# A perceiver layer on one core: context groups turned by TensorE, score sums taken inside the products, sums moved between VectorE, GpSimd and ScalarE

## The chip, the core and the metric

The kernel runs on one core of a Trainium2 chip. The metric is the device time of one execution in microseconds (us), as the median of several runs. The core's engines have a queue each and run side by side: TensorE (PE in the profile, its weight loads PEld), VectorE (DVE), ScalarE (ACT), GpSimd (POOL) and SyncE (SP), which here only issues DMAs. Everything is float32.

## The reference, cut to what matters

A layer of three parts works on 256 query tokens `x` of width 512: a cross attention with 25,088 context tokens, a causal self attention with 16 heads, and a mixture of experts. The change lies in the first part:

```python
x = x + _L0_xattn_ref(_layernorm(x), ctx_1024, ctx_1024, Wq, bq, Wk, bk, Wv, bv)

def _L0_xattn_ref(q, k, v, Wq, bq, Wk, bk, Wv, bv):
    qp = q @ Wq.T + bq            # 256 x 128
    kp = k @ Wk.T + bk            # 25088 x 128
    vp = v @ Wv.T + bv            # 25088 x 512
    z = sigmoid(qp @ kp.T / sqrt(128))   # 256 x 25088, no softmax
    return z @ vp
```

Since no softmax is taken, `z @ (ctx @ Wv.T + bv)` is `(z @ ctx) @ Wv.T + rsum * bv`, where `rsum` is the sum of each query's row of `z`. The kernel computes `z @ ctx` over all tokens, projects once at the end, and needs `rsum` for the bias.

## The kernel before

**The loop over groups.** The context is cut into 66 groups. Group 0 has 128 tokens (one block), each of groups 1 to 65 has 384 (three blocks of 128). For each group `g` the kernel does this:

- `load_quarters(g)` (line 119, four DMAs) loads the tokens cut into quarters of 512 bytes over the partitions, and `load_context(g)` (line 128) loads them again as they are, tokens on partitions. Both are issued by SP, three groups ahead in the loop; there are 3 buffers of quarters and 5 of context.
- `turn(g)` (line 315) turns the quarters on VectorE, by blocks of 32 x 32, into `cT`, with model width on partitions. Group 0 alone goes another way: `turn_by_pe(0)` (lines 317 to 329) turns its block from the context tile with four TensorE transposes and one ScalarE copy. The quarters have another order of rows than a plain transpose, so `keys` takes the weights `wkT_sb` for them, and `wk_plain_sb` for group 0.
- `keys(g)` (line 339) multiplies `cT` by the key weights, and ScalarE adds the bias (line 348). This gives `kT`.
- `scores` (line 360) multiplies `kT` by the queries `qT`, and ScalarE writes the sigmoid as `zT` (line 369), tokens on partitions.
- `context_sums` and `query_sums` (line 501) form sums of parts, and `values` (line 527) multiplies them. Here `z @ ctx` is a product of 2 x 3 blocks (`a00` to `a12`: two halves of the queries by three token blocks) and 3 x 3 blocks (`b00` to `b22`: three token blocks by three thirds of the width, 172 or 170 columns). A scheme with 15 products in place of 18 is used: each product `p0` to `p14` multiplies a block or sum of blocks of `zT` (`s0` to `s9`) by a block or sum of blocks of the context (`t0` to `t12`). The 15 products are summed over all groups in six PSUM banks. The `s` sums are all on VectorE; of the 13 `t` sums VectorE makes 6 and GpSimd 7.
- `summed` (line 379) adds the whole `zT` to `zsum` on GpSimd, for `rsum`.

**The order of the work.** Each engine's instructions run in program order. In iteration `g` the program issues, per engine:

- PE: scores of `g` for two blocks, the first four products of group `g-1`, scores for the third block, keys of `g+1`, the other eleven products of `g-1`
- DVE: `t` sums of `g`, `s` sums of `g`, turn of `g+2`
- POOL: seven `t` sums of `g`, then `zsum`, and in five groups some one-element copies (line 159) that hold back the DMAs of later weights
- ACT: the two sigmoids of `g`, the bias of `kT` for `g+1`

`t` sums have two buffers, so those of group `g` can be written only when the products of `g-2` have been read.

**Start and end.** Before the loop PE warms up (line 244), turns group 0 (line 324) and the normalised `x` (line 555), computes the keys of group 0 and the queries (line 565); on VectorE `turn(1)` stands ahead of `qT` (line 575). After the loop the last products run, ScalarE copies five of the six banks to SBUF (line 624), and the 15 products are combined into the six blocks `c00` to `c12` of the result by 21 additions (line 645), six of them on GpSimd. The first half is turned by PE (line 652), copied by ACT (line 657) and projected (line 690), then the second half. `rsum` comes from `zsum`: two GpSimd additions (lines 609 and 610), PE products with a column of ones (line 666), and a copy (line 675), used at line 679.

Of the kernel before, what the change touches and what calls it, by code (L numbers as in the profile page):

```python
# [14 lines left out]
P = 128  # L15
# [6 lines left out]
def tile_perceiver_layer(  # L22
# [84 lines left out]
    def blocks_of(g):  # L107

        return range(J) if g > 0 else (1,)
# [23 lines left out]


    x_sb = act.tile([P, NT, D], F32, tag="x", name="x_sb")
    for t, queue in enumerate((nc.sync, nc.scalar)):
# [5 lines left out]
    bq_sb = load("bq", [QK, 1], bq, queue=nc.gpsimd)  # L142
    load_quarters(1)
    wkT_sb = const.tile([P, ND, QK], F32, tag="wkT", name="wkT_sb")
    for a in range(NA):
# [3 lines left out]
        )  # L149
    load_context(1)  # L150

# [165 lines left out]
    def turn_by_pe(g):  # L317

        cT = new_turned(g)
        pt = sum_bank(f"ptc_{g}")  # L320
        ct = ctx_tiles[g][:, 1, :]
        for c in range(ND):
            chunk = slice(c * P, (c + 1) * P)
            in_turn(nc.tensor.transpose(pt[:, chunk], ct[:, chunk], ident))
        in_turn(
            nc.scalar.copy(
                cT[:, :, 0 : P // R, :], pt.rearrange("p (c b r) -> p c b r", c=ND, r=R)
            )
        )

    def keys(g):

        cT = turned_tiles.pop(g)
        n = len(blocks_of(g)) * P
        w = wkT_sb if g > 0 else wk_plain_sb
        pk = keys_bank(f"pk_{g}")[:, 0:n]
        for c in range(ND):
            in_turn(
                nc.tensor.matmul(  # L339
                    pk,  # L340
                    lhsT=w[:, c, :],
                    rhs=cT[:, c, 0 : n // R, :].rearrange("p b r -> p (b r)"),
                    start=(c == 0),
                    stop=(c == ND - 1),
                )
            )
        kT = cpool.tile([QK, J * P], F32, tag="kT", name=f"kT_{g}")
        in_turn(nc.scalar.activation(kT[:, 0:n], pk, AF.Identity, bias=bk_sb))  # L348
        return kT

    zsum = cpool.tile([P, J, T], F32, tag="zsum", name="zsum", bufs=1)
    nc.gpsimd.memset(zsum, 0.0)

# [22 lines left out]

    def summed(g, zT):
        part = slice(blocks_of(g)[0], blocks_of(g)[-1] + 1)
        in_turn(nc.gpsimd.tensor_add(zsum[:, part, :], zsum[:, part, :], zT[:, part, :]))  # L379

# [24 lines left out]
        t11 b02 - t0  # L405
        t12 b11 + t7
        t8 t2 + t4
    """
    T_SUMS_BY_POOL = """
        t1 b10 + b12  # L410
        t3 t1 - b22
        t4 b20 - t3
        t9 b02 + t1
        t5 b12 - b22
        t10 t5 - b11
        t6 b11 - b02
    """

    PRODUCTS = (
        ("p6 s2 t3", "p14 s0 t8", "p8 s5 b11"),  # L420
        ("p13 s6 b02", "p11 s8 t6"),
        ("p5 a12 b20", "p1 a01 t10", "p7 s1 t2"),
        ("p0 s9 b22", "p9 a00 t11"),
        ("p10 a10 b00", "p4 s7 b21"),
        ("p12 s4 t9", "p3 a11 b10", "p2 s3 t12"),
    )
    FIRST_S_SUMS = "s4 a11 + a01"
    FIRST_T_SUMS = """
        t1 b10 + b12
        t10 b12 - b11  # L430
    """
    FIRST_PRODUCTS = (
        ("p6 a01 t1", "p8 a11 b11"),
        ("p11 s4 b11",),
        ("p1 a01 t10",),
        (),
        (),
        ("p12 s4 t1", "p3 a11 b10"),
    )

    RESULTS = """
# [3 lines left out]
        u9 u6 - p7  # L445
        u13 p1 + u1
        u2 u1 - p9
        | u15 u9 - p5
        u4 p1 + u2
        | c02 p0 + u13  # L450
        u8 p7 - p10
        c01 u2 - p4
        | c00 u15 - u4
        u3 p2 + p4
        u11 p12 - p0
        | u7 p8 + u3
        u5 p3 + p13
        u10 p3 + p5
        | u14 u11 - p6
        c10 p10 + u10  # L460
        c11 u7 + u8
        | c12 u14 - u5
    """

    WIDE = ("p2", "p4", "p7", "p8", "p9", "p10", "p11", "p13")
    NS_SUMS, NT_SUMS, NU_SUMS = 10, 13, 16
    product, banks_of_products = {}, []

    def open_products():
        for i, names in enumerate(PRODUCTS):  # L470
            held = sum_bank(f"xacc_{i}")
            banks_of_products.append(held)
            at = 0
            for text in names:
                nm = text.split()[0]
                width = WIDTH if nm in WIDE else WIDTH - 2
                product[nm] = (i, slice(at, at + width))
                at += width

    class Named:  # L480


        def __init__(self, g):
            self.g = g
            self.s = self.t = self.z = None

        def __getitem__(self, nm):
            kind, at = nm[0], nm[1:]
            if kind == "a":
                i, k = int(at[0]), int(at[1])  # L490
                return self.z[:, k, i * P : (i + 1) * P]
            if kind == "b":
                lo = third_at[int(at[1])]
                return ctx_tiles[self.g][:, int(at[0]), lo : lo + WIDTH]
            return (self.s if kind == "s" else self.t)[:, int(at), :]

    def do_sums(engine, text, named):
        for line in text.strip().splitlines():
            to, x_, op, y_ = line.split()
            f = engine.tensor_add if op == "+" else engine.tensor_sub  # L500
            in_turn(f(named[to], named[x_], named[y_]))  # L501

    def context_sums(g, named):
        named.t = cpool.tile([P, NT_SUMS, WIDTH], F32, tag="T", name=f"T_{g}")
        if g == 0:
            do_sums(nc.vector, FIRST_T_SUMS, named)
        else:
            do_sums(nc.gpsimd, T_SUMS_BY_POOL, named)
            do_sums(nc.vector, T_SUMS, named)

# [6 lines left out]
    def values(named, lo=0, hi=15):  # L517
        g = named.g
        made = [
            (i, text.split(), text is names[-1])  # L520
            for i, names in enumerate(PRODUCTS if g > 0 else FIRST_PRODUCTS)
            for text in names
        ]
        for i, (nm, lhs, rhs), last in made[lo:hi]:
            cols = product[nm][1]
            in_turn(
                nc.tensor.matmul(  # L527
                    banks_of_products[i][:, cols],
                    lhsT=named[lhs],
                    rhs=named[rhs][:, 0 : cols.stop - cols.start],  # L530

# [27 lines left out]
    for i, copy in enumerate((nc.vector.tensor_copy, nc.scalar.copy)):  # L559
        in_turn(copy(xnT[:, 2 * i : 2 * i + 2, :].rearrange("p c t -> p (c t)"), pxs[i]))  # L560
    kT = keys(0)
    pq = sum_bank("pq")
    for c in range(ND):
# [8 lines left out]
        )  # L572
    turn(1)
    qT = cpool.tile([QK, T], F32, tag="qT", name="qT", bufs=1)
    in_turn(nc.vector.tensor_scalar(qT, pq[:, :T], bq_sb, None, ALU.add))  # L575
    open_products()
    load_quarters(2)
    load_context(2)


    before = None
    for g in range(G):
        if g + 3 < G:
            load_quarters(g + 3)
            load_context(g + 3)
        named = Named(g)
        named.z = zT = cpool.tile([P, J, T], F32, tag="zT", name=f"zT_{g}", bufs=3)
# [11 lines left out]
        query_sums(g, named)  # L599
        if g + 2 < G:  # L600
            turn(g + 2)
        summed(g, zT)
        for fetch in in_group.get(g, ()):
            fetch(zT[0:1, 0, 0:1])
        before = named
    values(before)


    in_turn(nc.gpsimd.tensor_add(zsum[:, 0, :], zsum[:, 0, :], zsum[:, 1, :]))
    in_turn(nc.gpsimd.tensor_add(zsum[:, 0, :], zsum[:, 0, :], zsum[:, 2, :]))  # L610

# [14 lines left out]
    def result(nm):  # L626
        if nm[0] == "p":
            i, cols = product[nm]
            widths[nm] = cols.stop - cols.start
            return banks_of_products[i][:, cols] if i == len(PRODUCTS) - 1 else held[i][:, cols]  # L630
# [5 lines left out]
    for line in RESULTS.strip().splitlines():  # L636
        engine = nc.gpsimd if "|" in line else nc.vector
        to, x_, op, y_ = line.replace("|", "").split()
        a_, b_, o_ = result(x_), result(y_), result(to)
        n = widths[to] = min(widths[x_], widths[y_])  # L640
        assert to not in ("c01", "c11") or n == WIDTH
        if to[0] == "c" and to[2] != "1":
            n = WIDTH - 2
        f = engine.tensor_add if op == "+" else engine.tensor_sub
        in_turn(f(o_[:, 0:n], a_[:, 0:n], b_[:, 0:n]))
    zcT = work.tile([P, ND, T], F32, tag="tokT", name="zcT")

# [14 lines left out]
    turn_zc(0, sum_bank)  # L662
    pr = sum_bank("pr")
    for t in range(NT):
        in_turn(
            nc.tensor.matmul(
                pr[:, t : t + 1],
                lhsT=zsum[:, 0, t * P : (t + 1) * P],
                rhs=ones_sb,
                start=True,  # L670
                stop=True,
            )
        )
    rsum = act.tile([P, NT], F32, tag="rsum", name="rsum")
    in_turn(nc.vector.tensor_copy(rsum, pr[:, 0:NT]))
    x1 = act.tile([P, NT, D], F32, tag="x1", name="x1")
# [854 lines left out]
```

## Time and profile before

| What | us |
|---|---|
| median of 3 runs | 795.2 (793.04 to 795.24) |
| the profiled execution, its own time | 796.75 |
| its span, first to last instruction | 794.9 |
| PE busy | 775.6 (98%) |
| DVE busy | 636.8 (80%) |
| POOL busy | 400.1 (50%) |
| ACT busy | 157.8 (20%) |
| DMA | 141.62 MB, 178 GB/s over the span |

The profiled execution is 1.85 us longer than its span, and 1.55 us longer than the median of the runs. The span falls into these stages by the timeline: start to the keys of group 3 at 30.47 us; the even loop to the keys of group 65 at 541.48 us; its end, with the last products, to about 561.2 us; the projection, self attention and experts to 794.9 us. Busy times on PE are modelled at their ends, and a VectorE instruction whose record is stretched counts as busy for all of it.

### The profile page before, as it was taken

Reading aid. Unit: us, or ns where it says so; the run is one execution under the profiler, and the core shown is the slowest. Engines: PE = TensorE matmul, PEld = TensorE weight load, DVE = VectorE, ACT = ScalarE, POOL = GpSimd, SP = SyncE. Lnnn points to the kernel's source line nnn. Section 1 sums busy time; section 2 is a strip of 40 time slices with the busy share of each in tenths; the row PEclk is TensorE's granted clock in tenths of the full one; section 3 lists DMA queues with packets and bytes.
Section 4 is the critical chain, followed back from the end, with each engine's and each line's share of the span. In section 5 each row is a group of like instructions: output and inputs, shape, how many; then the busy total and the mean of one; then the engine's idle time right before and its main releaser. Section 6 shows DMA issues by size and latency. Waiting matters only on the chain.

```text
span 794.9 us, 11690 instructions
## 1 busy us (share of the span) xinstructions
PE 775.6 (98%) x3994; PEld 609.6 (77%) x3994; DVE 636.8 (80%) x1389; ACT 157.8 (20%) x350; POOL 400.1 (50%) x574
## 2 busy tenths in 40 slices
PE   7999999999999999999999999999999899999996
PEld 4788888888888888888888888888675586775562
DVE  4899999999999999999999999999556463512222
ACT  2211112111121121212111121111445220110110
POOL 4576767767676676767767677676323000000000
PEclk8999999999999999999999999999999999999999
DMA  9998997997778787777878778730510033399400
GB/s 241 269 238 215 304 228 231 247 232 209 183 195 202 172 212 175 206 191 184 206 169 210 185 196 198 170 113 1 190 50 1 0 133 111 127 353 393 154 2 30
DMA packets 155251, 141.62 MB, mean 178 GB/s; under 512 B 9137, under 2 KB 114609, under 8 KB 155185
## 3 DMA queue, kind: packets, MB, share of 16 engines
q1 hardware_dynamic: 154448, 140.28, 66.7%
q8 instruction: 34, 0.56, 0.3%
q10 hardware_dynamic: 672, 0.52, 0.2%
q14 instruction: 33, 0.26, 0.1%
q0 software_dynamic: 64, 0.00, 0.0%
HBM read 140.25 MB, written 0.52 MB: 177 GB/s over the span
## 4 chain that ended last, share of the span: by engine, by line
DVE 52%; PE 40%; DMA 3%; issue 2%; POOL 1%; ACT 1%; SPq 0%; DVEq 0%; POOLq 0%; ACTq 0%
DVE T L501 27%; DVE S L501 13%; DVE cT L315 11%; PE xacc L527 7%; PE ph_e L1089 7%; PE pk L339 5%; PE pd_e L1136 3%; DMA quarters<-in_context 3%; PE ph_s L1089 3%; PE pz L360 2%; PE pd_s L1136 2%; PE pa L804 2%; PE ph_few L1358 1%; PE pw L868 1%; PE py L690 1%
## 5 line engine op out<-in xcount | busy, mean ns | idle before, releaser
L501 POOL TENSOR_TENSOR T<-ctx 128x172 f32<-128x172 f32 x195 | 124.0, 636 | 143.7 <-PE xacc L527 143.7
L501 DVE TENSOR_TENSOR T<-ctx,T 128x172 f32<-128x172 f32 x195 | 190.6, 1003 | 2.2
L339 PE MATMUL pk<-cT,wkT_sb 128*128 128x384 f32 x520 | 181.3, 492 | 0.9 <-DVE cT L315 0.8
L527 PE MATMUL xacc<-T,S 128*128 128x170 f32 (+1 forms) x782 | 167.4, 309 | 0.9 <-DVE S L501 0.9
L527 PEld LDWEIGHTS xacc<-T,S 128*128 128x128 f32 x782 | 134.1, 191 | 21.6 <-POOL zsum L379 1.2
L339 PEld LDWEIGHTS pk<-cT,wkT_sb 128*128 128x128 f32 x520 | 96.6, 192 | 61.3 <-DVE cT L315 2.5
L379 POOL TENSOR_TENSOR zsum<-zsum,zT 128x768 f32<-128x768 f32 (+1 forms) x66 | 123.9, 1877 | 14.4 <-ACT zT L369 14.4
L369 ACT ACTIVATE zT<-pz 128x256 f32<-128x256 f32 (+1 forms) x131 | 64.1, 489 | 286.1 <-PE pz L360 282.7
L315 DVE STREAM_TRANSPOSE cT<-quarters 128x1536 f32<-128x1536 f32 x65 | 115.1, 1771 | 5.8 <-DMA quarters<-in_context 5.8
L360 PE MATMUL pz<-qT,kT 128*128 128x256 f32 x392 | 106.7, 381 | 3.7 <-DVE qT L575 2.8
L527 PE MATMUL xacc<-ctx,S 128*128 128x172 f32 (+1 forms) x522 | 108.9, 310 | 0.4 <-DVE S L501 0.4
L527 PE MATMUL xacc<-ctx,zT 128*128 128x170 f32 (+1 forms) x394 | 89.5, 309 | 0.0
L527 PEld LDWEIGHTS xacc<-ctx,S 128*128 128x128 f32 x522 | 85.0, 191 | 0.9 <-DVE S L501 0.9
L501 DVE TENSOR_TENSOR T<-ctx 128x172 f32<-128x172 f32 x132 | 81.5, 618 | 0.0
L501 DVE TENSOR_TENSOR S<-zT,S 128x128 f32<-128x128 f32 x325 | 78.8, 292 | 0.0
L360 PEld LDWEIGHTS pz<-qT,kT 128*128 128x128 f32 x392 | 68.8, 190 | 8.9 <-issue 3.2
L501 POOL TENSOR_TENSOR T<-T,ctx 128x172 f32<-128x172 f32 x130 | 67.5, 519 | 10.2
L501 POOL TENSOR_TENSOR T<-ctx,T 128x172 f32<-128x172 f32 x130 | 65.9, 528 | 5.1
L348 ACT ACTIVATE kT<-pk,bk 128x384 f32<-128x384 f32 (+1 forms) x66 | 38.1, 577 | 151.9 <-PE pk L339 151.9
L527 PEld LDWEIGHTS xacc<-ctx,zT 128*128 128x128 f32 x394 | 66.3, 191 | 0.0
L501 DVE TENSOR_TENSOR S<-zT 128x128 f32<-128x128 f32 x196 | 57.9, 296 | 3.3 <-ACT zT L369 3.3
L527 PE MATMUL xacc<-T,zT 128*128 128x170 f32 (+1 forms) x264 | 60.2, 310 | 0.0
(238 smaller groups left out, 722.0 us busy)
## 6 DMA issues: line engine op xcount, KB each, us to landing
quarters<-in_context SPq DMA_DIRECT2D x260, 192.0 KB, 5.0
ctx<-in_context SPq DMA_DIRECT2D x65, 768.0 KB, 5.3
gu<-in_e_gate_up SPq DMA_DIRECT2D x12, 1024.0 KB, 7.3
dn<-in_e_down SPq DMA_DIRECT2D x11, 512.0 KB, 4.9
gu_s<-in_s_gate_up SPq DMA_DIRECT2D x8, 512.0 KB, 6.3
a_wqT<-in_a_wqT SPq DMA_DIRECT2D x1, 2048.0 KB, 8.1
a_wout<-in_a_woutT SPq DMA_DIRECT2D x1, 2048.0 KB, 9.2
dn_s<-in_s_down SPq DMA_DIRECT2D x4, 512.0 KB, 8.3
```

What stands on the lines that cost most here:

```text
L315: in_turn(nc.vector.transpose(new_turned(g), q.rearrange("p b (c r) -> p c b r", r=R)))
L339: nc.tensor.matmul(pk, lhsT=w[:, c, :], rhs=cT[:, c, 0 : n // R, :].rearrange("p b r -> p (b r)"), start=(c == 0), stop=(c == ND - 1),)
L348: in_turn(nc.scalar.activation(kT[:, 0:n], pk, AF.Identity, bias=bk_sb))
L360: nc.tensor.matmul(pz[:, i * T : (i + 1) * T], lhsT=kT[:, at : at + P], rhs=qT, start=True, stop=True,)
L369: nc.scalar.activation(zT[:, blocks[0] : blocks[-1] + 1, :].rearrange("p j t -> p (j t)"), pz[:, 0 : len(blocks) * T], AF.Sigmoid, scale=1 ...
L379: in_turn(nc.gpsimd.tensor_add(zsum[:, part, :], zsum[:, part, :], zT[:, part, :]))
L501: in_turn(f(named[to], named[x_], named[y_]))
L527: nc.tensor.matmul(banks_of_products[i][:, cols], lhsT=named[lhs], rhs=named[rhs][:, 0 : cols.stop - cols.start],  start=i not in opened, ...
L690: nc.tensor.matmul(pys[t], lhsT=zcT[:, c, t * P : (t + 1) * P], rhs=wvT_sb[:, c, :], start=(c == 0), stop=(c == ND - 1),)
L804: nc.tensor.matmul(pa[:, 0 : hi - lo], lhsT=a_wqT_sb[:, c, e * P : (e + 1) * P], rhs=anT[:, c, lo:hi], start=(c == 0), stop=(c == ND - 1),)
L1089: nc.tensor.matmul(ph[:, f * T + lo : f * T + hi], lhsT=gu[:, c, col : col + P], rhs=fT[:, c, lo:hi], start=(c == 0), stop=(c == ND - 1),)
L1136: nc.tensor.matmul(pd, lhsT=hT[:, f, t * P : (t + 1) * P], rhs=dn[:, f, :], start=(f == 0), stop=(f == NI - 1),)
```

## The change

**Start.** Groups 0 and 1 (`BY_PE = 2`) are turned by TensorE. `turn_by_pe` now takes groups of three blocks: 12 transposes into four PSUM banks, each bank copied out by ACT or DVE in turn. The quarters of group 1 are not loaded; its context is loaded where its quarters were, and the quarters of group 2 come next. `qT` comes ahead of the turn of group 1 on its engines. `keys(1)` takes `wk_plain_sb`. One sigmoid of a single column is put behind the copies of `xnT` on ScalarE.

**Score sums.** The `t` tiles are two fixed ones, 174 columns wide, whose last columns are set to 1.0 once. The products `p0`, `p9`, `p10` and `p12` get one more column, which reads a one: it sums the product's `s` or `a` operand over the tokens. `p0` and `p10` used a block of the context itself, which has no ones beside it, so ScalarE copies these two blocks to `t13` and `t14`. `summed`, `zsum` and all that made `rsum` of it are taken out; `rsum` is three one-column operations on VectorE.

**The sums.** `t5`, `t10` and `t6` go from GpSimd to VectorE: 9 there, 4 on GpSimd. GpSimd's four and ScalarE's two copies for group `g+1` are issued at the end of iteration `g` (`context_sums_aside`). `t1` shares the place of `t10`. The products are laid out in the banks anew, and issued in another order of banks except in the last group.

**End.** The 21 additions of the result are all on VectorE, in another order.

The diff, cut to its core:

```diff
+    BY_PE = 2
...
-    load_quarters(1)
+    load_context(1)
+    load_quarters(2)
     wkT_sb = const.tile([P, ND, QK], F32, tag="wkT", name="wkT_sb")
...
-    load_context(1)
+    load_context(2)
...
     def turn_by_pe(g):
         cT = new_turned(g)
...
+        blocks = blocks_of(g)
+        n = len(blocks)
+        many = 512 // (n * P)
+        for lo in range(0, ND, many):
+            pt = sum_bank(f"ptc_{g}_{lo}")[:, 0 : many * n * P]
+            for c in range(lo, lo + many):
+                for i, k in enumerate(blocks):
+                    at = ((c - lo) * n + i) * P
+                    in_turn(
+                        nc.tensor.transpose(
+                            pt[:, at : at + P],
+                            ctx_tiles[g][:, k, c * P : (c + 1) * P],
+                            ident,
+                        )
+                    )
+            to = cT[:, lo : lo + many, 0 : n * P // R, :]
+            src = pt.rearrange("p (c b r) -> p c b r", c=many, r=R)
+            if lo % 2:
+                in_turn(nc.vector.tensor_copy(to, src))
+            else:
+                in_turn(nc.scalar.copy(to, src))
...
-        w = wkT_sb if g > 0 else wk_plain_sb
+        w = wkT_sb if g >= BY_PE else wk_plain_sb
...
-    def summed(g, zT):
-        part = slice(blocks_of(g)[0], blocks_of(g)[-1] + 1)
-        in_turn(nc.gpsimd.tensor_add(zsum[:, part, :], zsum[:, part, :], zT[:, part, :]))
...
     T_SUMS = """
...
+        t5 b12 - b22
+        t10 t5 - b11
+        t6 b11 - b02
         t8 t2 + t4
     """
     T_SUMS_BY_POOL = """
         t1 b10 + b12
         t3 t1 - b22
+        t9 b02 + t1
         t4 b20 - t3
-        t9 b02 + t1
-        t5 b12 - b22
-        t10 t5 - b11
-        t6 b11 - b02
     """
+    T_COPIES_BY_ACT = "t13 b22, t14 b00"
...
-        ("p0 s9 b22", "p9 a00 t11"),
-        ("p10 a10 b00", "p4 s7 b21"),
-        ("p12 s4 t9", "p3 a11 b10", "p2 s3 t12"),
+        ("p9 a00 t11", "p4 s7 b21"),
+        ("p12 s4 t9", "p3 a11 b10", "p0 s9 t13"),
+        ("p10 a10 t14", "p2 s3 t12"),
     )
...
-        ("p12 s4 t1", "p3 a11 b10"),
+        ("p12 s4 t9", "p3 a11 b10", "p0 a01 t13"),
...
+    BANK_ORDER, LAST_ORDER = (0, 1, 2, 4, 3, 5), range(6)
+    SCORE_SUMS = ("p0 + p9", "p12 - p0 + p10")
+    WITH_ONES = ("p0", "p9", "p10", "p12")
...
-                width = WIDTH if nm in WIDE else WIDTH - 2
+                width = (WIDTH if nm in WIDE else WIDTH - 2) + (nm in WITH_ONES)
...
+    t_tiles = []
+    for i in range(2):
+        t = cpool.tile([P, NT_SUMS, WIDTH + 2], F32, tag=f"T{i}", name=f"T_{i}", bufs=1)
+        nc.vector.memset(t[:, :, WIDTH - 2 :], 1.0)
+        t_tiles.append(t)
+    nc.vector.memset(t_tiles[0][:, 13, 0 : WIDTH - 2], 0.0)
...
+    def context_sums_aside(g, named):
+        if g == 0:
+            return
+        do_sums(nc.gpsimd, T_SUMS_BY_POOL, named)
+        for line in T_COPIES_BY_ACT.split(", "):
+            to, x_ = line.split()
+            n = WIDTH - 2 if to in NARROW_T else WIDTH
+            in_turn(nc.scalar.copy(named[to][:, 0:n], named[x_][:, 0:n]))
...
+    warm = small.tile([P, 1], F32, tag="warm", name="warm_0", bufs=1)
+    in_turn(nc.scalar.activation(warm, eps_sb, AF.Sigmoid))
     kT = keys(0)
...
-    turn(1)
     qT = cpool.tile([QK, T], F32, tag="qT", name="qT", bufs=1)
     in_turn(nc.vector.tensor_scalar(qT, pq[:, :T], bq_sb, None, ALU.add))
+    turn_by_pe(1)
     open_products()
-    load_quarters(2)
-    load_context(2)
...
         query_sums(g, named)
-        if g + 2 < G:
+        if BY_PE <= g + 2 < G:
             turn(g + 2)
-        summed(g, zT)
         for fetch in in_group.get(g, ()):
             fetch(zT[0:1, 0, 0:1])
-        before = named
+        before, named = named, Named(g + 1)
+        if g + 1 < G:
+            context_sums_aside(g + 1, named)
     values(before)
-    in_turn(nc.gpsimd.tensor_add(zsum[:, 0, :], zsum[:, 0, :], zsum[:, 1, :]))
-    in_turn(nc.gpsimd.tensor_add(zsum[:, 0, :], zsum[:, 0, :], zsum[:, 2, :]))
...
-        engine = nc.gpsimd if "|" in line else nc.vector
...
+    rsum = act.tile([P, NT], F32, tag="rsum", name="rsum")
+    for t, text in enumerate(SCORE_SUMS):
...
+            in_turn(f(rsum[:, t : t + 1], total, result(nm)[:, -1:]))
...
-    pr = sum_bank("pr")
-    for t in range(NT):
-        in_turn(
-            nc.tensor.matmul(
-                pr[:, t : t + 1],
-                lhsT=zsum[:, 0, t * P : (t + 1) * P],
-                rhs=ones_sb,
...
-    in_turn(nc.vector.tensor_copy(rsum, pr[:, 0:NT]))
```

## The prediction

> **What bounds the kernel now.** I read the chain of waits first, because busy shares alone (PE 98%, VectorE 80%) don't say which engine sets the pace. Then the windows by stage, then the timeline of one group and of both ends.
>
> The chain names VectorE for half of the span and PE for most of the rest. In an early stretch it stays on PE for a whole group (start, length, what):
>
> ```profile
> 38.97 2.58 PE pk L339 x8
> 41.55 3.19 PE xacc L527 x22
> 44.74 0.86 PE pz L360 x4
> 45.60 1.16 PE xacc L527 x8
> 46.76 0.43 PE pz L360 x2
> ```
>
> These five pieces follow each other without a gap and add up to 8.22 us. That is PE's own work for a group. The windows (length, then busy time of PE, PEld, DVE, ACT, POOL, then clock and DMA):
>
> ```profile
> 11.08:13.92 2.84, 0.01 (x2) 0.03 (x1) 2.29 (x3) 0.00 (x0) 0.00 (x0) 0.88 1.08 312
> 13.92:20.22 6.30, 6.29 (x10) 3.13 (x10) 2.16 (x4) 0.38 (x1) 4.19 (x8) 0.51 1.16 272
> ...
> 30.47:541.48 511.01, 510.92 (x2729) 431.62 (x2730) 506.74 (x1055) 96.35 (x185) 355.61 (x504) 1.00 0.81 202
> ...
> 553.06:561.21 8.15, 6.80 (x30) 5.97 (x30) 5.69 (x15) 2.51 (x5) 3.52 (x5) 0.79 0.00 0
> ```
>
> Over the even loop PE is busy 510.92 of 511.01 us and VectorE 506.74: both are full. The keys of group 3 start it and those of group 65 end it, so it holds 62 groups at 511.01/62 = 8.242 us, 0.02 over PE's own 8.22. So PE is the floor, and VectorE just keeps up. The other rows show PE idle or at half clock, at both ends. VectorE's fullness is partly waiting, as the timeline of one group shows:
>
> ```profile
> 181.00 2.48 DVE L501 TENSOR_TENSOR T<-ctx,T 128x172 f32<-128x172 f32 x2
> 181.38 1.90 POOL L379 TENSOR_TENSOR zsum<-zsum,zT 128x768 f32<-128x768 f32 x1
> ...
> 183.40 0.33 DVE L501 TENSOR_TENSOR T<-T 128x172 f32<-128x172 f32 x1
> 183.65 0.28 DVE L501 TENSOR_TENSOR S<-zT 128x128 f32<-128x128 f32 x1
> ```
>
> Two sums take 2.48 us beside `zsum`; with GpSimd quiet, one starts 0.25 us after another (183.40, 183.65), and an `S` sum 0.20 us (177.16, 177.36).
>
> **The change part by part.** I count against the profiled execution (796.75 us; span 794.9).
>
> *Start.* In the timeline the queries end on PE at 11.08, and then:
>
> ```profile
> 11.62 1.78 DVE L315 STREAM_TRANSPOSE cT<-quarters 128x1536 f32<-128x1536 f32 x1 [2.99 <-DMA quarters<-in_context]
> ...
> 13.33 0.44 DVE L575 TENSOR_SCALAR qT<-pq,bq 128x256 f32<-128x256 f32 x1
> ```
>
> `qT` stands behind the turn of group 1, which waits for quarters. PE idles 2.83 us, its clock falls to half, and keys of group 1 take 5.12 us instead of 2.58. After the change `qT` is ready at 11.55. The context of group 1 (0.77 MB) is the fifth load, after 1.3 MB; with the 207 GB/s of the first window, 2.1 MB are there at 10.2 us. Bounds: 9.5, at the rate of other context loads (about 2.2 us each beside 3.5 for a group's quarters), and 11.6, when the quarters landed in that place. I take 10.2. From 11.08 PE makes 12 transposes at 0.11 each (the four of group 0 and the four at 562.27 both), 1.4 us. Each bank's copy costs ACT or DVE about 0.5 (0.59 for 512 columns); two each, the first three under the transposes. PE then runs pz of group 0 (0.43), keys 1 (2.58, from 12.95), a gap for kT (0.65, as before), pz 0.86, four products 1.16, pz 0.43: keys 2 at 18.65. Those need turn 2: its quarters landed at 18.7 before, behind those of group 1, `wkT` and the context; now they follow the context by 3.3 us of DMA, at 13.5, so `cT` is ready at about 15.6, and `wkT` lands at about 15.5. Then keys 2.58, three products 0.87, pz 0.86, four products 1.16, pz 0.43: keys 3 at 24.55. Turn 3 needs quarters that landed at 24.4 before; 0.77 MB less ahead of them makes 21.2, and after the `s` sums (21.1) `cT` is ready at 23.0. Gain 30.47 - 24.55 = 5.9 us; with quarters 3 as late as before, 4.3.
>
> The added memsets, about 0.4 us on VectorE, lie in its wait for `x` (2.88 us idle before line 254); without that cover they would cost 0.4. The early sigmoid puts the 1.28 us table load ahead of kT of group 0, which then ends at 10.7, before 12.45: nothing, and nothing gained, as the load was covered at 9.78 too. SP issues four DMAs fewer (2.77 us); its load of context 4 waits for group 0's products as before (now about 22), with quarters 5 behind it, not read before 39; POOL loses the `zsum` memset (0.73), off the path.
>
> Here a rule of the skill speaks against the change. The row: clock 0.88 between 11.08 and 13.92, that is a fall to half at about 13.24, 2.2 us after the last matmul. The Trainium skill, "TensorE: Matmul & The Clock Gate", Part 4, says that transposes don't count as PE work for the clock. By the row alone PE has work from 11.08 on and stays at full clock. By the rule it rests from 11.08 to 12.45, 1.4 us, or to 13.0 with the late landing: near 2.2. A fall would repeat the 6.3 us at half clock, about 3 us lost. I take the row, 1.4 being under 2.2, and keep 3 us as the upper end.
>
> *The even loop.* PE: four more columns, each in two passes (a matmul is recorded twice) at 0.145/172 us a column: 4 x 2 x 0.84 ns = 7 ns a group, x65 = +0.4 us. The order of banks costs nothing. VectorE: minus `zsum`'s hold, plus three sums. 10 `S` at 0.20, turn 1.70, nine `T` at 0.25 makes 5.95; beside GpSimd's four sums a `T` sum takes 0.6 instead (timeline 179.26 to 181.00), so at most 4 x 0.35 = 1.4 more: 7.4 of 8.22 us. VectorE then waits for PE. What is left of the 0.02 us a group goes, 62 x 0.02 = -1.2. Net -0.8. GpSimd falls from about 5.6 to 2.3 us of work a group. ACT's two copies, at most 0.4 each (0.38 for 256 columns), stand in its queue ahead of the next sigmoid and wait for p10, next to last of a group. They end about 0.5 us into the next iteration, while the sigmoid waits for pz until 0.86. Cover 0.36 us; beyond that zT, then the `S` sums, come later, and these have about 4 us before PE reads them. GpSimd's four sums wait for the products of `g-1`, as its seven did; behind them stand only the copies at line 159. VectorE's t10 waits for t9, GpSimd's third, and t8 for its fourth; the `S` sums queue behind, but they need zT, 2.85 us into the iteration, while four of GpSimd's at 0.6 end at 2.4. DMA: quarters of groups 4 to 18 landed 5 us or more ahead of their turn; the start brings PE 5.9 us and the loads 3.2 us forward, which leaves 2.8.
>
> *The last group.*
>
> ```profile
> 551.97 3.02 DVE L501 TENSOR_TENSOR S<-zT,S 128x128 f32<-128x128 f32 x4
> ...
> 554.00 0.81 PE L527 MATMUL xacc<-T,S 128*128 128x170 f32 x4 [0.95 <-DVE S L501]
> ...
> 561.47 0.75 POOL L645 TENSOR_TENSOR zc<-u 128x170 f32<-128x170 f32 x1 [0.34 <-DVE u L645]
> 562.27 0.66 PE L652 MATMUL pt_zc<-ident,zc 128*128 128x128 f32 x4 [1.06 <-POOL zc L645]
> ```
>
> The last `S` sums sit behind `zsum`, PE waits for them, and after that runs at half clock (0.79 over the row). By the pieces above, keys 65 (2.58), eleven products (3.19), the iteration without keys (5.64) and fifteen products (4.35) should take 15.76 us from 541.48, which is 557.24; it took until 561.21. After the change the sums of this group, with all four of GpSimd's in their way, start at 0.5 in the iteration and end by 4.2; the `S` sums by 6.2, the first ones in time for PE at 5.64. Gain 3.95. If they still are late by 1 us and the clock falls, 1.5.
>
> *The result.* VectorE takes the six sums of GpSimd, at 0.25 to 0.35 each. Its chain to c02 ends about 0.8 us after the last product, where the first transpose stood 1.06 after. Gain 0.3. The second half (ten sums, then three for `rsum`, 3.5 us) is ready before PE turns to it (3.9). The products and copy of the old `rsum` were covered by ACT's copy: nothing.
>
> Sum: -5.9 -0.8 -3.95 -0.3 = -10.95. The profiled time would be 785.8; the median of 795.2, 784.3.
>
> **The rivals.** (a) The start gains less: the clock falls during the transposes (+3) or quarters 3 are late (+1.6). For it: the rule, and a DMA share over 1 in these windows. Against it: the short rest. It gives about 787.3. (b) The last group still waits, +2.5: 786.8. For it: nine sums now on VectorE ahead of the `S` sums; against it: no `zsum`. (c) Slower: VectorE becomes the bound, as it gets three sums more where the loop left it little room. If all nine `T` sums cost the 0.62 of today's contended ones, a group takes 9 x 0.62 + 2.05 + 1.70 = 9.3 us, 1.1 over PE's floor, x64 = +70, about 854. It decides from 8.4 us a group on, where 0.17 x 64 eats the gain. Against it: GpSimd has only four sums to stand in the way, not nine. (d) It doesn't do what it says: freeing GpSimd moves nothing because PE sets the pace anyway. In the even loop that is my forecast; at both ends PE does wait.
>
> **How the numbers follow.** Forecast 0.68 (own range 782 to 786), (a) 0.17, (b) 0.10, (c) and other new waits in the loop 0.05, of which 0.02 end within 0.3% (2.4 us, what a measurement can tell). The runs before spread by 2.2 us. The range reaches from 781.5 (landing early, no cost of the ones) to 789 (both (a) and part of (b)). Faster 0.95, same 0.02, slower 0.03.
>
> **What would show it.** Keys 3 start near 24.5 with the clock at 1.0 throughout; 62 groups take 8.23 us each, PE full, VectorE under 90% busy; no PE gap between the last two groups' products; first zc transpose under 1 us after the last product. A clock of 0.5 between 12 and 20 speaks for (a), a wait of PE for `S` near 545 for (b), 8.3 us or more a group with VectorE full for (c).

## The result and the profile after

The changed kernel takes 792.0 us (median of 8 runs, 791.3 to 792.98); the kernel before takes 794.53 us in 8 runs (793.04 to 795.37). The ratio is 0.997, with a 95% interval from 0.9959 to 0.9981. The kernel is faster, by 2.5 us; about 11 were forecast. The profiled execution takes 792.2 us with a span of 790.3 us, 4.6 us below the 794.9 of before.

Engine totals first, then the chain that ended last, both from the page of the changed kernel:

```profile
PE 769.8 (97%) x4004; PEld 611.3 (77%) x4004; DVE 548.3 (69%) x1596; ACT 202.3 (26%) x483; POOL 154.4 (20%) x304
...
PE 95%; DVE 2%; ACT 1%; DMA 0%; POOL 0%; issue 0%; ACTq 0%
```

GpSimd fell from 400 to 154 us and VectorE from 637 to 548. Before, the chain ran through VectorE for half of the span (52%); now it is PE for 95%. By these two lines the work moved as the change says. Where the time went is seen only by stage. The windows of the changed kernel (length, then busy time of PE, PEld, DVE, ACT, POOL, then clock, DMA share and GB/s), cut at the first product of PE, the transposes of group 1, the start of the keys of group 3 ("keys 3" from here on), keys 65, the end of the last product and the first projection product:

```profile
0.00:8.28 8.28, 0.00 (x1) 0.01 (x1) 3.83 (x16) 1.87 (x3) 3.47 (x16) 1.00 0.69 221
8.28:16.83 8.55, 8.55 (x34) 5.67 (x35) 0.69 (x1) 2.92 (x5) 1.86 (x4) 1.00 1.16 278
16.83:30.59 13.76, 13.09 (x66) 10.13 (x65) 11.71 (x33) 5.11 (x12) 1.92 (x4) 1.00 1.18 268
30.59:541.05 510.46, 510.46 (x2729) 434.96 (x2728) 425.39 (x1244) 138.30 (x310) 129.31 (x258) 1.00 0.85 200
541.05:557.00 15.95, 15.95 (x97) 14.47 (x95) 9.81 (x38) 5.22 (x11) 2.06 (x4) 1.00 0.00 1
557.00:559.08 2.08, 0.70 (x5) 0.45 (x4) 2.01 (x9) 0.63 (x2) 0.00 (x0) 1.00 0.00 0
```

The rows from the second to the fifth show PE full or nearly so, and the granted clock is 1.00 in all six. The first row is the surprise: PE does nothing for 8.28 us. Against the profiled execution of before, stage by stage:

| Stage | before, us | after, us | difference | forecast |
|---|---|---|---|---|
| start to keys 3 | 30.47 | 30.59 | +0.12 | -5.9 |
| 62 groups | 511.01 | 510.46 | -0.55 | -0.8 |
| keys 65 to the end of the last product | 19.73 | 15.95 | -3.78 | -3.95 |
| from there to the first projection product | 2.40 | 2.08 | -0.32 | -0.3 |
| the rest of the span | 231.29 | 231.22 | -0.07 | 0 |

Three terms came out near their forecasts. The largest one, the start, is missing altogether. The timeline of PE in the changed kernel shows why:

```profile
8.28 4.72 PE L246 MATMUL pi<-idle_sb 128*128 128x512 f32 x6 [8.28 <-DVE idle_sb L241]
12.83 0.60 PE L332 MATMUL ptc<-ident,ctx 128*128 128x128 f32 x4
...
15.11 1.89 PE L611 MATMUL pq<-xnT,wqT 128*128 128x256 f32 x8
16.83 1.47 PE L332 MATMUL ptc<-ident,ctx 128*128 128x128 f32 x12
...
18.58 2.74 PE L353 MATMUL pk<-cT,wk_plain 128*128 128x384 f32 x8
```

In the kernel before, the same engine had these lines:

```profile
1.60 5.21 PE L244 MATMUL pi<-idle_sb 128*128 128x512 f32 x6 [1.60 <-DVE idle_sb L239]
...
9.19 1.89 PE L565 MATMUL pq<-xnT,wqT 128*128 128x256 f32 x8
13.92 1.19 PE L360 MATMUL pz<-qT,kT 128*128 128x256 f32 x2 [2.83 <-DVE qT L575]
14.90 5.31 PE L339 MATMUL pk<-cT,wkT_sb 128*128 128x384 f32 x8
```

The first line of each is the warm-up (`keep_warm`), which multiplies a tile of zeros. It is the first product in PE's program, and in this trace no product ran ahead of it (0.00 us of PE work in the first 8.28). Its bracket names what it waited for: the memset of `idle_sb` on VectorE. From the transposes of group 1 to keys 3 (30.59) the new start then runs as forecast: 13.76 us, where the prediction had 24.55 - 11.08 = 13.47. But it runs about 6 us late. The memset in the timelines of VectorE, before and then after:

```profile
1.06 0.48 DVE L239 MEMSET idle_sb<- 128x512 f32 x1
```

```profile
7.14 0.55 DVE L587 TENSOR_SCALAR xn<-x_sb,mv_x,rs_x 128x512 f32<-128x512 f32 x1
7.74 0.48 DVE L241 MEMSET idle_sb<- 128x512 f32 x1
```

It has moved from the first microseconds to behind the last instruction of the normalisation of `x`. The diff doesn't touch the memset, and the trace shows no wait of its own ahead of it. It isn't among the instructions whose order the kernel fixes with `in_turn`, and its tile is in the ring of five context buffers (tag `ctx`), in which the changed kernel allocates one more context tile ahead of it.

### The profile page after: what moved, and what is told of

It reads as the page before. It is cut to its first block, busy times and chain, and to the rows that moved or that the text cites. A ratio compares the mean times of both kernels' runs of the same rounds, so it can differ in the third digit from the quotient of the medians.

```text
span 790.3 us, 12132 instructions
## 1 busy us (share of the span) xinstructions
PE 769.8 (97%) x4004; PEld 611.3 (77%) x4004; DVE 548.3 (69%) x1596; ACT 202.3 (26%) x483; POOL 154.4 (20%) x304
## 4 chain that ended last, share of the span: by engine, by line
PE 95%; DVE 2%; ACT 1%; DMA 0%; POOL 0%; issue 0%; ACTq 0%
PE xacc L570 36%; PE pk L353 21%; PE pz L371 11%; PE ph_e L1124 7%; PE pd_e L1171 4%; PE ph_s L1124 3%; PE pd_s L1171 2%; PE pa L839 2%; PE ph_few L1393 1%; PE pw L903 1%; PE py L725 1%; PE ps L929 1%; PE ptp L980 1%; PE po_few L1424 1%; PE pf L1370 1%; PE pd_few L1438 1%
## 5 line engine op out<-in xcount | busy, mean ns | idle before, releaser
L570 PE MATMUL xacc<-T,S 128*128 128x172 f32 (+2 forms) x912 | 185.5, 308 | 0.0
L537 DVE TENSOR_TENSOR T<-ctx 128x172 f32<-128x172 f32 (+1 forms) x262 | 113.5, 434 | 0.0
L537 POOL TENSOR_TENSOR T<-ctx 128x172 f32<-128x172 f32 x65 | 32.0, 493 | 391.3 <-PE xacc L570 373.5
L570 PE MATMUL xacc<-T,zT 128*128 128x173 f32 (+1 forms) x396 | 89.9, 308 | 0.0
L570 PE MATMUL xacc<-ctx,S 128*128 128x172 f32 x392 | 78.5, 309 | 0.0
L547 ACT COPY T<-ctx 128x170 f32<-128x170 f32 (+1 forms) x130 | 43.2, 334 | 125.4 <-PE xacc L570 125.4
L537 POOL TENSOR_TENSOR T<-ctx,T 128x170 f32<-128x170 f32 (+1 forms) x130 | 72.4, 576 | 2.2 <-PE xacc L570 2.2
L537 DVE TENSOR_TENSOR T<-ctx,T 128x172 f32<-128x172 f32 x195 | 65.5, 361 | 8.2 <-PE xacc L570 1.5
L570 PEld LDWEIGHTS xacc<-T,zT 128*128 128x128 f32 x396 | 66.4, 190 | 0.1
L1124 PE MATMUL ph_e<-fT,gu 128*128 128x256 f32 x256 | 57.9, 381 | 0.0
```

The lines of the kernel that those rows point to most:

```text
L537: in_turn(f(o_, a_, b_))
L547: in_turn(nc.scalar.copy(named[to][:, 0:n], named[x_][:, 0:n]))
L570: nc.tensor.matmul(banks_of_products[i][:, cols], lhsT=named[lhs], rhs=named[rhs][:, 0:n],  start=i not in opened, stop=(g == G - 1 and last),
L1124: nc.tensor.matmul(ph[:, f * T + lo : f * T + hi], lhsT=gu[:, c, col : col + P], rhs=fT[:, c, lo:hi], start=(c == 0), stop=(c == ND - 1),)
```

## Experiments

My theory: the memset's new place costs about 6 us, and everything else is as forecast. The rivals: the start would not have gained anyway (something else ends there at 30.5, for example the quarters of group 3); or the moved sums brought a loss that hides a gain.

**e1: the zeros come first.** The tile and its memset are moved ahead of all loads, so that no context tile precedes them:

```diff
     BY_PE = 2
+    idle_sb = cpool.tile([P, J, D], F32, tag="ctx", name="idle_sb", bufs=5)[:, 0, :]
+    nc.vector.memset(idle_sb, 0.0)
     x_sb = act.tile([P, NT, D], F32, tag="x", name="x_sb")
...
-    idle_sb = cpool.tile([P, J, D], F32, tag="ctx", name="idle_sb", bufs=5)[:, 0, :]
-    nc.vector.memset(idle_sb, 0.0)
```

> The changed kernel, but the zeroed tile that the warm-up multiplies is made ahead of all context tiles, so its memset comes first on VectorE. Theory (the start's gain was lost because PE's whole queue stood behind the warm-up, and that behind a memset that had moved to 7.74 us): warm-up from about 1.6 us as before, keys of group 3 at 24.0 to 25.0 us, median 6 us under the changed kernel, about 786. Rival (the start is bound by the loads, the late memset was covered): keys of group 3 at 28 or later with VectorE waiting for quarters, median 790 to 792. Second rival (the clock falls during the transposes): clock 0.5 in a stretch of 12 to 20 us, median about 789.

Measured: 785.78 us (785.56 to 785.93), ratio to before 0.9885 (0.9871 to 0.99). That is 6.2 us below the changed kernel. PE's timeline in this kernel:

```profile
1.47 4.62 PE L246 MATMUL pi<-idle_sb 128*128 128x512 f32 x6 [1.47 <-DVE idle_sb L137]
...
12.57 2.74 PE L353 MATMUL pk<-cT,wk_plain 128*128 128x384 f32 x8
...
18.54 2.74 PE L353 MATMUL pk<-cT,wkT_sb 128*128 128x384 f32 x8
...
24.58 2.74 PE L353 MATMUL pk<-cT,wkT_sb 128*128 128x384 f32 x8
```

Keys 3 start at 24.58; the prediction had 24.55. The span is 784.0 us, 10.9 below before's profiled 794.9; the forecast sum was 10.95. By the stages of the table it is -5.89, -0.55, -3.77 and -0.33, and -0.36 in the rest, for which nothing was forecast; by medians of the runs it is -9.05. So the stages gain about what was predicted once the memset is early, and the late place of one unchanged instruction had cancelled the gain of the start.

**e6: one line's order.** Is it the place of the memset among the loads that decides? The changed kernel with its memset where it was, and only the load of context 2 put behind it:

```diff
-    load_context(2)
...
     nc.vector.memset(idle_sb, 0.0)
+    load_context(2)
```

> The changed kernel, with one line moved: the load of context group 2 comes behind the zeroed tile in the program instead of ahead of it. Theory (the memset went late because its tile waits its turn in the ring of context tiles behind that load): memset before x is normalised, as in e1, median 785.5 to 786.5. Rival (it went late because of the new memsets of ones, or the early memset of e1 helps by having another buffer): 790 or more.

Measured: 786.0 us (785.69 to 786.48), ratio 0.9891 (0.9875 to 0.9908). VectorE's timeline has the memset early again:

```profile
1.39 0.48 DVE L240 MEMSET idle_sb<- 128x512 f32 x1
```

It stands right behind the memsets of the `t` tiles, the warm-up starts at 1.93, and keys 3 start at 24.53. With two context tiles ahead of `idle_sb` (before and here) the memset is early; with three (the changed kernel) it is late. So the new memsets alone don't make it late, since they are here too. Why the load of one more context tile does, the tile's place in the ring or the order in which the program's instructions are laid out, cannot be read in a profile and stays open.

**e2: the late zeros in the kernel before.** The same delay, without the change; the call that issues the warm-up goes behind the memset:

```diff
-    nc.vector.memset(idle_sb, 0.0)
...
-    keep_warm(3)
...
+    in_turn(nc.vector.memset(idle_sb, 0.0))
+    keep_warm(3)
     turn_by_pe(0)
```

> The kernel before, with nothing changed but the place of the same memset: behind the normalisation of x, where the changed kernel had it. Theory (a late warm-up costs only what is not covered; here PE idled 2.8 us and ran keys of group 1 at half clock for 2.6 us more, which a later warm-up fills and speeds up): keys of group 3 at 30 to 32 us, median 0 to +1.5 us. Rival (a late memset costs its 6.2 us wherever it stands): keys of group 3 at 36.5, median +6.

Measured: 795.64 us (13 runs, 794.73 to 798.0), ratio 1.0014 (1.0004 to 1.0024): +0.8 us for a delay that costs the changed kernel 6.2. PE's timeline, with the two lines in which PE waits between the queries and keys 3 for VectorE:

```profile
17.70 0.67 PE L359 MATMUL pz<-qT,kT 128*128 128x256 f32 x2 [0.67 <-DVE qT L575]
18.21 2.74 PE L338 MATMUL pk<-cT,wkT_sb 128*128 128x384 f32 x8
...
31.21 2.20 PE L338 MATMUL pk<-cT,wkT_sb 128*128 128x384 f32 x6 [0.84 <-DVE cT L314]
```

In the kernel before, PE idled 2.83 us before these scores and then ran at half clock. With a late warm-up it arrives there later, idles 0.67 us, and never loses its clock (1.00 from 0 to 31.21; keys of group 1 take 2.74 us in the timeline, not 5.31). The delay fills the idle time and saves the slow stretch. In the changed kernel these two are gone already, so the delay is paid in full. Its queries start 5.92 us later than before's (15.11 against 9.19), and from there to keys 3 it takes 5.80 us less (15.48 against 21.28). That the two have the same size is chance. It holds only for the execution of before that was shown: in that of e7, keys 3 start at 28.51, which is 2.1 us ahead of the changed kernel.

**e3: only group 1 turned the old way.** The rest of the change and the early zeros kept:

```diff
-    BY_PE = 2
+    BY_PE = 1
...
-    load_context(1)
-    load_quarters(2)
+    load_quarters(1)
...
-    load_context(2)
+    load_context(1)
...
+    turn(1)
     qT = cpool.tile([QK, T], F32, tag="qT", name="qT", bufs=1)
     in_turn(nc.vector.tensor_scalar(qT, pq[:, :T], bq_sb, None, ALU.add))
-    turn_by_pe(1)
     open_products()
+    load_quarters(2)
+    load_context(2)
```

> As e1, but only group 0 is turned by TensorE; the loads and the turn of group 1 stand as in the kernel before. Theory (turning group 1 by TensorE is worth 5.9 us once the warm-up is early): keys of group 3 near 30.5, clock 0.5 between 13 and 20 us, median 5 to 6 us over e1. Rival (the early memset alone makes the start fast): within 1 us of e1.

Measured: 789.51 us (789.1 to 790.38), ratio 0.9931 (0.9918 to 0.9944), so 3.7 us over e1. The old wait is back, in PE's timeline and in a window of the same columns as above:

```profile
13.62 1.19 PE L370 MATMUL pz<-qT,kT 128*128 128x256 f32 x2 [3.00 <-DVE qT L620]
14.61 5.22 PE L352 MATMUL pk<-cT,wkT_sb 128*128 128x384 f32 x8
```

```profile
13.20:19.60 6.40, 5.98 (x10) 3.21 (x10) 2.82 (x5) 0.38 (x1) 1.91 (x4) 0.50 1.16 284
```

Keys 3 start at 29.09, 4.5 us behind e1 and 1.4 ahead of before. The 5 to 6 us that were expected came out as 3.7 by medians; the profiled execution (790.38) is the slowest of the five. So of the 5.9 us that the start gains, 3.7 to 4.5 come from TensorE's turn of group 1 and its loads. The rest comes with other parts of the change: here the queries end 0.46 us earlier than before (10.62 against 11.08), and the wait of keys 3 for `cT` is gone (0.84 us in before and in e2). Which part does it was not tried.

**e8: does the clock outlast the transposes?** In before's profile the clock fell, by the prediction's estimate, 2.2 us after PE's last product. The prediction weighed against this row a rule of the Trainium skill ("TensorE: Matmul & The Clock Gate", Part 4) by which transposes don't count as PE work for the clock, and set it aside because 1.4 us of them is less than 2.2. By the row, longer transposes keep the clock; by the rule, they lose it. Here group 1's transposes are made three times over, each time with the same result:

```diff
-            for c in range(lo, lo + many):
+            for c in list(range(lo, lo + many)) * (3 if g == 1 else 1):
```

> As e1, with each of the 12 transposes of group 1 made three times (the second and third write the same numbers again): about 4.1 us with nothing but transposes on PE between the queries and the scores of group 0, longer than the 2.2 us of rest after which the clock fell in the kernel before. By the row of before (a PE with work keeps its clock): clock 1.0 throughout, keys of group 3 at 27.3, median +2.7 us. By the rule that transposes don't count as work for the clock: clock 0.5 from about 13 us on for 3 to 6 us, keys of group 1 in 4 to 5.2 us instead of 2.6, median +4.5 to +6.

Measured: 788.59 us (788.2 to 789.38), ratio 0.9928 (0.9905 to 0.9951): +2.8 us over e1, which is the added transposes themselves (24 x 0.11 = 2.6). The windows over the transposes alone, and from there to keys 3:

```profile
10.60:14.54 3.94, 3.94 (x38) 3.93 (x37) 1.04 (x2) 0.96 (x2) 1.63 (x4) 1.00 1.21 236
14.54:26.98 12.44, 11.77 (x55) 8.82 (x54) 10.67 (x31) 4.15 (x10) 1.91 (x4) 1.00 1.15 289
```

Transposes alone fill 3.94 us, longer than the idle times with which the clock fell in before (2.83), e7 (2.58) and e3 (3.00), and it stays at 1.00 in both windows. For these float32 transposes, coming to a clock that is already full, the rule isn't borne out; the row was the right guide. Whether they could raise a halved clock was not tried.

**e5: the three sums back on GpSimd.** This is e1 with `t5`, `t10` and `t6` moved back:

```diff
-        t5 b12 - b22
-        t10 t5 - b11
-        t6 b11 - b02
         t8 t2 + t4
...
+        t5 b12 - b22
+        t10 t5 - b11
+        t6 b11 - b02
```

> As e1 (785.8 us), with t5, t10 and t6 back on GpSimd: it makes seven sums, VectorE six. Theory (PE is the floor of the loop and VectorE has about 1.7 us of room a group without zsum, wherever these three sums are): 62 groups at 8.22 to 8.24 us, VectorE under 90% busy, median within 0.5 us of e1. Rival (the three sums had to leave GpSimd, which would hold VectorE up again): 8.25 us or more a group with waits of PE for S or cT, median +1.5 us or more.

Measured: 786.04 us (785.82 to 786.68), ratio 0.9889 (0.9872 to 0.9905); 0.26 us over e1, with overlapping ranges (e1 goes up to 785.93). The loop's window:

```profile
25.29:535.76 510.47, 510.47 (x2730) 434.96 (x2729) 433.33 (x1057) 138.18 (x310) 230.41 (x444) 1.00 0.86 204
```

The 62 groups take 510.47 us, 0.01 more than e1. GpSimd is busy 230 us where e1 has 129, and VectorE 433 where e1 has 425, though it makes three sums fewer a group. The `t` sums left to it stretch beside GpSimd: by kind they take 552 to 610 ns on average, in e1 330 to 437. Neither engine sets the pace, so once `zsum` is gone this part of the change is worth nothing in the loop. (Keys 3 start 0.7 us later in this profile because two loads landed later: PE waited 0.45 us for `wk_plain` and 0.24 for the context of group 1.)

**e10: no columns of ones.** This is e1 with the score sums left out, so that the bias is scaled by the wrong numbers:

```diff
-    WITH_ONES = ("p0", "p9", "p10", "p12")
+    WITH_ONES = ()
```

> As e1, without the four columns of ones (the sums of scores are left out; three one-column operations read other numbers in their place). Theory (PE is the floor, so 4 columns in 2 passes at 0.84 ns are paid in full): median -0.3 to -0.6 us. Rival (the loop is held by something else): within 0.1 us.

Measured: 785.39 us (785.35 to 785.53), ratio 0.9882 (0.9866 to 0.9899), 0.39 us below e1:

```profile
24.50:534.56 510.06, 510.06 (x2730) 434.55 (x2729) 425.12 (x1245) 138.17 (x310) 128.98 (x258) 1.00 0.85 204
```

The loop is 0.40 us shorter than e1's 510.46. The prediction priced four more columns at 7 ns a group, +0.4 us.

**e9: the final sums as before.** This is e1 with the old order of the 21 additions (the reordered list is left out here), six of them on GpSimd again:

```diff
-        f = nc.vector.tensor_add if op == "+" else nc.vector.tensor_sub
+        f = engine.tensor_add if op == "+" else engine.tensor_sub
```

> As e1, with the 21 additions of the result in the order and on the engines of the kernel before (six on GpSimd). Theory (moving them to VectorE is worth 0.2 to 0.4 us on the way to the first transpose): last product to first projection product 2.4 to 2.6 us instead of 2.2, median +0.2 to +0.4. Rival (it is covered): within 0.1 us.

Measured: 786.28 us (786.21 to 786.58), ratio 0.9894 (0.9877 to 0.991), 0.5 us over e1, where 0.2 to 0.4 were expected. PE's timeline shows the first transpose of the result waiting for GpSimd, where e1's waits 0.70 us for VectorE:

```profile
552.26 0.66 PE L700 MATMUL pt_zc<-ident,zc 128*128 128x128 f32 x4 [1.31 <-POOL zc L684]
```

**e4: the kernel before, without its last `zsum`.** Only the addition of the last group is left out, so the bias lacks that group's scores:

```diff
-        summed(g, zT)
+        if g < G - 1:
+            summed(g, zT)
```

> The kernel before, with the score sum of the last group left out (its 384 tokens are missing in the sum of scores, nothing else). Theory (in the last group the zsum addition holds up the S sums, PE waits and its clock falls): no PE gap over 0.3 us before the last fifteen products, these at full clock, keys of group 65 to last product 15.8 to 16.3 us instead of 19.7, median -2 to -4 us. Rival (PE waits for the nine or ten sums themselves, not for zsum): gap and half clock stay, within 0.5 us of before.

Measured: 792.87 us (22 runs, 791.37 to 795.12), ratio 0.9978 (0.997 to 0.9985), 1.96 us less than before, just under the 2 to 4 expected. The window from keys 65 to the end of the last product:

```profile
540.17:556.60 16.43, 16.29 (x97) 14.46 (x95) 15.27 (x39) 4.44 (x9) 10.00 (x15) 1.00 0.01 1
```

It takes 16.43 us where before's profile has 19.73 and the changed kernel 15.95, with PE nearly full (16.29) at clock 1.00. So one GpSimd addition of 1.9 us held back the last `S` sums, and through them PE, as the prediction read it. The profiled gain (3.3) is larger than the median's (1.96); e7 shows a reason.

**e7: the kernel before, once more.** This is one more execution, with nothing changed:

> The kernel before, once more, for another profile. Theory (the waits at both ends are the same in each execution, but whether and how long the clock falls differs, and this is the spread of its times): PE idle of 2.6 to 3 us before the scores of group 0 and about 0.9 before the last products, but other lengths of half clock than 6.3 and about 4 us. Rival (the profile shown is typical): the same lengths within 0.5 us.

Measured: 792.92 us in a single run, span 791.1. The windows of its start, and of its last two groups' products:

```profile
10.63:13.39 2.76, 0.18 (x2) 0.03 (x1) 2.29 (x3) 0.15 (x1) 0.00 (x0) 0.97 1.08 336
13.39:16.64 3.25, 3.25 (x6) 2.15 (x7) 0.64 (x3) 0.38 (x1) 1.41 (x3) 0.50 1.24 240
...
551.05:558.00 6.95, 5.31 (x31) 4.38 (x30) 5.86 (x16) 2.50 (x5) 3.33 (x5) 1.00 0.01 2
```

PE waits in the same places (2.58 us for `qT`, 0.75 for the last `S` sums; 2.83 and 0.95 in before's profile), but after the start's wait it runs at half clock for 3.25 us, where the profile of before had 6.3, and at the end there is no half clock (1.00 against 0.79). Keys 65 to the first projection product take 20.71 us here, 22.13 in before's profile, 18.03 in the changed kernel. So the same wait can cost a different amount in each execution. The runs on record point the same way: of 35 runs of before, the 20 with a mean granted clock of 0.996 have a median of 793.8 us, the 15 with a lower one (0.992 to 0.994) 795.0. This isn't the whole of the spread: the changed kernel, whose profile has no half clock, still ranges over 1.7 us in 8 runs.

## Why the prediction was wrong, step by step

**Start: the step that failed.** The forecast of -5.9 took everything that PE does ahead of 11.08 us as it stood, and so put any shift of it at nothing, without a reason. Of VectorE it costed only the memsets that the change adds (0.4 us, in the wait for `x`), and of the reordered loads only the DMAs. That a load of one more context tile, written ahead of `idle_sb`, could shift an unchanged memset on another engine was not considered. It shifted by 6.7 us (1.06 to 7.74), the warm-up with it, and PE's first transposes from 6.65 to 12.83. The start measured +0.12. With the memset early the numbers of the step hold within 0.4 us, in e1: keys 1 at 12.57 (forecast 12.95), the wait for kT 0.67 (0.65), keys 2 at 18.54 (18.65), keys 3 at 24.58 (24.55). The quarters of groups 2 and 3 came in time, the context of group 1 only just: GpSimd's first sum of it waited for it until 10.87, where 10.2 was forecast. Why the load moves the memset stays open (e6).

**The clock.** The choice of the row over the rule was right (e1, e8). Its 2.2 us is not a fixed figure, though: in e4 the clock fell about 3.0 us after the queries ended (last section).

**The even loop.** Forecast -0.8, measured -0.55, at 510.46/62 = 8.233 us a group. VectorE is busy 425.39/62 = 6.86 us a group, inside the forecast 5.95 to 7.4, and waits in nearly every group for the sigmoid:

```profile
DVE S L537 <- ACT zT L380: 72.7, 64, 1.4
```

(engine, tile and line, releaser; then total us, times, longest.) The cost of the ones was exact (e10). That GpSimd's relief bought the loop almost nothing was forecast too (e5).

**The last group.** Forecast -3.95, measured -3.78 between the profiled executions, and e4 confirms the cause. But that size belongs to an execution whose clock fell; to the first projection product the gain is 22.13 - 18.03 = 4.1 us against it, and 20.71 - 18.03 = 2.7 us against e7.

**The result.** Forecast -0.3, measured -0.32 in the stage; e9 puts the new sums at 0.5 us. The first transpose stood 0.70 us behind the last product, forecast 0.8.

**From the profile to the median.** The prediction took its whole gain off a profiled execution 1.55 us over the median known then, and carried that distance over. By 8 runs it was 2.2 over (796.75 against 794.53). Its mean granted clock was 0.991, lower than in any of the 35 runs above, so at least part of the distance is half clock, and a kernel that removes the half clock removes that part too. e1's profiled execution is on its median (785.76 and 785.78). So for a kernel without such stretches the forecast of 785.8 on the profile's own basis was the better number; 784.3 takes 1.5 us of it off twice.

**The rivals.** (a) was wrong in both halves, the clock and the quarters, although a start that gains too little was where the time was lost. (b): PE has no wait in the last group (window 541.05 to 557.00). (c): VectorE did not become the bound. (d), that freeing GpSimd moves nothing, holds in the loop, as forecast, and for the three moved sums (e5). It does not hold at the end, where `zsum` (e4) and the final sums (e9) had cost time.

The fastest version that still makes the whole result is e1, 785.78 us; e6, with 786.0, is close to it.

## What to carry to other kernels

Before costing what a change adds, list what stands first in each engine's queue and what it depends on, and ask whether the change can move *that*, including instructions it doesn't touch; where order isn't fixed by hand, a line added ahead can move what follows. When a large change brings little, compare the two timelines from the first microsecond: an early shift of everything and a shorter stage behind it can cancel, and only the starts of unchanged instructions show it. And when an execution holds half-clock stretches, their length is not a property of the kernel alone: take the gain of removing them from several executions, not from one.

## What the runs showed of the hardware

- After a PE wait of 2.6 to 3.0 us at the start the clock fell to half. Estimated from the clock of narrow windows of the traces, it was at half from 13.24 to 20.06 us in before, 12.76 to 19.59 in e3, 14.36 to 17.75 in e4 and 13.22 to 16.64 in e7. So it fell 2.1 to 3.0 us after PE's last product, and stayed there for about 6.8 us in before and e3 and 3.4 in e4 and e7; in the last group of before (0.79 over 8.15 us) it was about 3.4 too. What decides between 3.4 and 6.8 was not found.
- In the last group PE's first wait was 0.95 us in before, where the clock fell (0.79 over the row), and 0.75 in e7 and 0.82 in e2, where it stayed at 1.00.
- Float32 transposes alone, 3.94 us of them, left a granted clock of 1.00 at 1.00 (e8).
- A warm-up that starts 6 us late cost the kernel before 0.8 us (e2) and the changed kernel 6.2 (against e1): in the first it filled an idle time after which the clock had fallen.
- VectorE's `t` sums take longer beside GpSimd, so far that moving three sums of each group from VectorE to GpSimd raised VectorE's busy time, from 425.37 us in e1's loop to 433.33 (e5).
